# 21 matmuls on zeros in place of twelve ahead of the first product of the context

## The chip, the cores and the metric

The kernel runs on one core of a Trainium2 chip. The metric is the device time of one execution in microseconds (us); the figure to compare is the median of several executions. Before the change it is 1860.94 us, the median of three executions (1864.06, 1858.99 and 1860.94).

Five engines work side by side, each through its own instructions in order: TensorE (PE in the profile) multiplies, VectorE (DVE) and ScalarE (ACT) read and write SBUF and PSUM, GpSimd (POOL) works in SBUF, SyncE (SP) issues DMAs. An instruction that needs another engine's result carries a wait on a semaphore, and everything behind it on its own engine stands still until that wait ends.

## The reference, cut to what matters

The reference defines four sets of attention, but the context has just the 77 text positions, so the kernel computes cross-attention over those: 32 batches of 512 queries, 20 heads of 32 columns.

```
q = heads(x @ to_q_w)                      # x: 32 x 512 x 640
k = heads(ctx @ to_k_w)                    # ctx: 32 x 77 x 1024
v = heads(ctx @ to_v_w)
p = softmax(q k^T / sqrt(32))              # per head, over 77 keys
out = merge(p v) @ to_out_w + to_out_b + x
```

Float32 is required, so each operand is split into a high part and a rest, and each product is three matmuls (high by high, high by rest, rest by high).

## The kernel before, in words

**Keys and values of the whole context.** The 32 x 77 = 2464 rows of the context are cut into five groups: four of 512 rows and a last one of 416. The 1024 input columns are eight slices (index k), the 640 output columns five chunks (index j). One accumulator of keys or values, `pk` or `pv`, is one chunk of one group; it takes 8 x 3 matmuls (L204) and fills one PSUM bank. VectorE turns the context slices (L171), ScalarE and VectorE split them (L179, L183) and the weights (L103, L104).

**The first group** goes slice by slice, as the weights land: `first` (L339 to L354) runs, for one slice, 15 matmuls of keys (five chunks) and nine of values (three chunks). Eight accumulators are open at once. In groups 1 to 3 a whole group's keys are made in a row, and its values chunk by chunk. Finished values are turned by VectorE (`turn_values`, L256) into one of two buffers `vs` by turns, split there (L262, L266) and stored to DRAM by four DMAs (L271); finished keys are split (L225, L229) and stored (L235). The keys and values of the last groups are part of the next stage.

**The attention** runs by a list of tokens for each batch (`FILL`, `PLAN`, `LAST_`), which says in which order each step is issued; the order on every engine is the order of the tokens. `FILL` (L789) starts with the last values of group 3 (tokens YV, L204, tile `pv`), then has the keys of the last group (YJ, tile `pk`: digits j and k), the first query product (Yq, L542, tile `pq`) and the last group's values (YC), mixed with the first scores (L577), exponentials (L602), and so on. The token YJ30 is chunk 3, slice 0. It stands between YJ22 and YJ11. Among the SP tokens, Yx0 (the load of the second batch's `x`, L302) stands ahead of Ys20, the first of four stores of value chunk 2.

**The PSUM banks.** There are eight. Up to group 3 all `pk`, `pv` and the tile `warm` come from one pool of eight (L139), and which bank a new accumulator gets is decided while the program is recorded, by a timetable that the recorder keeps of its own; the order of instructions is fixed by hand (L327). From the last group on the banks are handed to new pools (`open_banks`, L437; `bank_of`, L429) by name: key chunk 3 and the first query accumulator each inherit one certain bank, and the first matmul into it has to wait until the accumulator that stood there before has been read.

**The matmuls on zeros.** Ahead of everything TensorE runs L336 and L337: a tile `zero` is set by VectorE, and matmuls of 128 x 512 on it write a tile `warm`, which nobody reads.

## Time and profile before

| what | value |
|---|---|
| median of three executions | 1860.94 us |
| the profiled execution | 1860.52 us |
| its span, first to last instruction | 1858.7 us |
| PE busy in the span | 1843.8 us (99%) |
| DVE, ACT, POOL busy | 1563.8, 1524.9, 1301.7 us |
| mean clock granted to TensorE | 0.999 of full |
| matmuls | 10332 |

The stages by time: matmuls on zeros 1.45 to 6.21 us; group 0 from 8.28 us; groups 0 to 3, keys and values, to 227.2 us; the start of the attention to about 380 us; from there the steady part. A row of the timeline has start, length, engine, line, operation, output and inputs, shape and count; in brackets is how long the engine sat idle ahead of it and what ended that. A matmul's length includes its tail, so consecutive ones overlap. A row of stretches has, per engine, busy time and count, then the clock granted to TensorE (PEclk, 1.00 is full speed), the DMA share and GB/s.

### The profile page before, as it was taken

Reading aid. Unit: us, or ns where it says so; the run is one execution under the profiler, and the core shown is the slowest. Engines: PE = TensorE matmul, PEld = TensorE weight load, DVE = VectorE, ACT = ScalarE, POOL = GpSimd, SP = SyncE. Lnnn points to the kernel's source line nnn. Section 1 sums busy time; section 2 is a strip of 40 time slices with the busy share of each in tenths; the row PEclk is TensorE's granted clock in tenths of the full one; section 3 lists DMA queues with packets and bytes.
Section 4 is the critical chain, followed back from the end, with each engine's and each line's share of the span. In section 5 each row is a group of like instructions: output and inputs, shape, how many; then the busy total and the mean of one; then the engine's idle time right before and its main releaser. Section 6 shows DMA issues by size and latency. Waiting matters only on the chain.

```text
span 1858.7 us, 37494 instructions
## 1 busy us (share of the span) xinstructions
PE 1843.8 (99%) x10332; PEld 1656.9 (89%) x10332; DVE 1563.8 (84%) x2502; ACT 1524.9 (82%) x6218; POOL 1301.7 (70%) x1120
## 2 busy tenths in 40 slices
PE   9999999999999999999999999999999999999999
PEld 7888897889999999999999999999999999999998
DVE  5444458899999999999999999999999999999996
ACT  3232248999999999999999999999999999999984
POOL 1100158787887787777778777887788878877874
PEclk9999999999999999999999999999999999999999
DMA  9879779889898888989988989899899988888875
GB/s 186 197 196 251 179 189 261 248 244 243 238 243 242 238 239 227 246 236 232 247 236 240 240 239 242 234 236 245 231 236 247 242 239 240 232 236 240 237 219 192
DMA packets 563295, 431.37 MB, mean 232 GB/s; under 512 B 191120, under 2 KB 471120, under 8 KB 563088
## 3 DMA queue, kind: packets, MB, share of 16 engines
q1 hardware_dynamic: 558192, 413.16, 84.6%
q0 software_dynamic: 4800, 15.65, 2.6%
q8 instruction: 85, 1.39, 0.3%
q14 instruction: 122, 1.00, 0.2%
q10 hardware_dynamic: 96, 0.16, 0.0%
HBM read 247.17 MB, written 181.64 MB: 231 GB/s over the span
## 4 chain that ended last, share of the span: by engine, by line
PE 93%; ACT 2%; DMA 1%; DVE 1%; SPq 1%; issue 1%; POOL 0%; DVEq 0%; ACTq 0%; POOLq 0%
PE po L750 30%; PE pq L542 28%; PE pa L694 12%; PE sc L577 11%; PE pk L204 6%; PE pv L204 6%; ACT pn L602 1%; DMA pd<-z 1%; SPq L531 0%; SPq L633 0%; DVE z L624 0%; POOL xt L320 0%; DMA v_dram<-vs 0%; DVE pp L672 0%; DMA cs<-in_ctx_dram 0%
## 5 line engine op out<-in xcount | busy, mean ns | idle before, releaser
L602 ACT ACTIVATE pn<-sc,nm 128x77 f32<-128x77 f32 x2560 | 795.8, 342 | 39.5 <-DVE nm L588 33.1
L750 PE MATMUL po<-wo_s,at 128*128 128x320 f32 x3840 | 708.1, 311 | 0.1
L750 PEld LDWEIGHTS po<-wo_s,at 128*128 128x128 f32 x3840 | 620.1, 189 | 41.5 <-DVE xr L765 0.6
L542 PE MATMUL pq<-xt,wq_s 128*128 128x512 f32 x2400 | 597.5, 394 | 1.1 <-DVE qt L787 0.8
L602 ACT ACTIVATION_READ_ACCUMULATOR pn<-sc,nm 128x1 f32 x2560 | 567.2, 222 | 0.0
L542 PEld LDWEIGHTS pq<-xt,wq_s 128*128 128x128 f32 x2400 | 436.6, 188 | 80.9 <-ACT pn L602 1.2
L617 POOL TENSOR_TENSOR pn<-pn,rs 128x1232 f32<-128x1232 f32 x160 | 388.0, 2425 | 91.2 <-DVE rs L612 87.5
L694 PE MATMUL pa<-pp,vb 128*128 128x512 f32 x960 | 341.6, 404 | 3.7 <-DVE at L731 2.0
L577 PEld LDWEIGHTS sc<-kb,qt 128*128 128x128 f32 x1920 | 303.9, 188 | 16.6 <-ACT pn L602 2.3
L588 DVE TENSOR_REDUCE nm<-sc 128x4 f32<-128x308 f32 x640 | 295.2, 466 | 23.0 <-PE sc L577 18.9
L577 PE MATMUL sc<-kb,qt 128*128 128x154 f32 (+1 forms) x1920 | 302.7, 274 | 2.7 <-ACT pn L602 1.9
L783 POOL CAST qt<-qt 64x512 fp32r<-64x512 f32 x320 | 196.8, 615 | 142.2 <-ACT qt L779 127.3
L712 DVE TENSOR_TENSOR pa<-pa,aw 64x512 f32<-64x512 f32 x320 | 222.1, 694 | 50.1 <-ACT aw L708 42.7
L624 DVE STREAM_TRANSPOSE z<-pn 128x1280 f32<-128x1280 f32 x160 | 241.1, 1507 | 14.1 <-DMA pd<-z 8.1
L679 POOL TENSOR_TENSOR pp<-raw,pp 64x512 fp32r<-64x512 f32 x160 | 206.7, 1292 | 64.7 <-ACT pp L661 56.1
L708 ACT COPY aw<-pa 64x1024 f32<-64x1024 f32 x160 | 162.1, 1013 | 88.4 <-PE pa L694 87.5
L787 DVE TENSOR_TENSOR qt<-pq,qt 64x512 fp32r<-64x512 f32 x320 | 216.6, 677 | 6.0 <-ACT qt L779 1.1
L320 POOL TENSOR_TENSOR xt<-xs,xt 128x512 fp32r<-128x512 f32 x160 | 203.6, 1300 | 20.0 <-ACT xt L316 15.2
L743 POOL TENSOR_TENSOR xr<-xr,bias 128x640 f32<-128x640 f32 x128 | 202.6, 1584 | 14.2 <-DMA xr<-in_x_dram 3.9
L672 DVE TENSOR_TENSOR pp<-raw,pp 128x1024 fp32r<-128x1024 f32 x160 | 196.2, 1226 | 0.0
L694 PEld LDWEIGHTS pa<-pp,vb 128*128 128x128 f32 x960 | 174.0, 189 | 14.9 <-ACT pp L663 2.8
L663 ACT CAST pp<-raw 128x1024 fp32r<-128x1024 f32 x160 | 168.5, 1053 | 1.0 <-DMA raw<-pd 1.0
(46 smaller groups left out, 1584.8 us busy)
## 6 DMA issues: line engine op xcount, KB each, us to landing
pd<-z SPq DMA_DIRECT2D x640, 160.0 KB, 3.3
raw<-pd SPq DMA_DIRECT2D x160, 512.0 KB, 4.5
xr<-in_x_dram SPq DMA_DIRECT2D x128, 320.0 KB, 3.8
out_dram<-xr SPq DMA_DIRECT2D x127, 320.0 KB, 3.7
xs<-in_x_dram SPq DMA_DIRECT2D x124, 320.0 KB, 5.9
raw<-pd SPq DMA_DIRECT2D x160, 128.0 KB, 4.1
v_dram<-vs SPq DMA_DIRECT2D x80, 192.0 KB, 4.1
k_dram<-ks POOLq DMA_DIRECT2D x20, 512.0 KB, 4.3
```

The costliest lines, as they stand in the source:

```text
L204: nc.tensor.matmul(held[j][:, :gn], w[:, k, a, :], cts[g, k][:, c, :gn], start=(k == 0 and n == 0), stop=(k == NK - 1 and n == 2),)
L542: nc.tensor.matmul(pqs[n], wq_s[:, k, a, j * P : (j + 1) * P], xts[b, k][:, c, :], start=(k == 0 and m == 0), stop=(k == NC_ - 1 and m == 2),)
L577: nc.tensor.matmul(sc[:, cols], qt[:, m, t * P : (t + 1) * P], keys_, start=(m == 0), stop=(m == 2),)
L588: nc.vector.tensor_reduce(nm, sc[:, :KCOLS].rearrange("p (h k) -> p h k", k=NKEY), AX.X, ALU.max, negate=True)
L602: nc.scalar.activation(pnb[n % 2][:, at, :NKEY], sc[:, i * NKEY : (i + 1) * NKEY], AF.Exp, bias=nm[:, i : i + 1], accum_out=sms[n][:, at : ...
L617: nc.gpsimd.tensor_tensor(pf, pf, rs.unsqueeze(2).to_broadcast([P, NQ * HPC, NKEY]), ALU.mult)
L624: nc.vector.transpose(z.rearrange("p b t j -> p t b j"), pn.rearrange("p (t h) k -> p t (h k)", t=NQ).rearrange("p t (b i) -> p t b i", i=Q),)
L679: nc.gpsimd.tensor_tensor(pp[64:, 4, :], raw[:64, 2, :], pp[:64, 4, :].bitcast(F32), ALU.subtract)
L694: nc.tensor.matmul(pas[n][:, p, :], vb[:, p, t, :], pp[:, c, :], start=(c == p), stop=(c == p + 2),)
L712: nc.vector.tensor_tensor(pa[64 * p : 64 * p + 64, 0], pa[:64, p], aw[:, p], ALU.add)
L750: nc.tensor.matmul(pos[b, t, h][:, :HALF], ats[b * NC_ + j][:, a, t * P : (t + 1) * P], wos[0][:, j, c, h * HALF : (h + 1) * HALF], start= ...
L787: nc.vector.tensor_tensor(qt[rows, 1 + w, :], pqs[n][rows], qt[rows, 0, :].bitcast(F32), ALU.subtract)
```

## The change

One number changes.

```
-    for _ in range(12):
+    for _ in range(21):
         nc.tensor.matmul(warm, zero[:, :P], zero, start=True, stop=True)
```

The order of the instructions on DVE, ACT, POOL and SP is the same in both programs, and so is what they wait for, except that counts of finished matmuls are higher by nine. On PE two places differ.

The first is the start of PE's program: the matmuls on zeros, then the first key products of group 0 (`wk_s_88` holds chunks 0 to 2 of the key weights).

```order
 L1123 UNCONDITIONAL_BRANCH [waits barrier_Pool_Activation_PE_DVE_SP_release]
 L337 MATMUL warm<-zero 128x512 [waits DVE_49]
-L337 MATMUL warm<-zero 128x512 x11
+L337 MATMUL warm<-zero 128x512 x20
 L204 MATMUL pk<-ct,wk_s_88 128x512 [waits Activation_49]
 L204 MATMUL pk<-ct,wk_s_88 128x512 [waits DVE_49] x2
```

Nine more matmuls stand ahead of the first product; it waits for ScalarE as it did.

The second place is the keys of the last group, in the start of the attention. Rows with `wk_s_89` are key chunks 3 and 4, and the first of these is YJ30. `DVE_49` is VectorE's count of finished work.

```order
 L204 MATMUL pk<-ct,wk_s_88 128x416 [waits Activation_49]
 L204 MATMUL pk<-ct,wk_s_88 128x416 x5
-L204 MATMUL pk<-ct,wk_s_89 128x416 x3
+L204 MATMUL pk<-ct,wk_s_89 128x416 [waits DVE_49]
+L204 MATMUL pk<-ct,wk_s_89 128x416 x2
 L204 MATMUL pk<-ct,wk_s_88 128x416 x3
 L204 MATMUL pk<-ct,wk_s_88 128x416 [waits Activation_49]
```

No instruction moved, but the first matmul of key chunk 3 now waits for VectorE. Further on, at the end of this run of keys, stands the first matmul of the first query accumulator.

```order
 L204 MATMUL pk<-ct,wk_s_89 128x416 x3
 L204 MATMUL pk<-ct,wk_s_88 128x416 [waits Activation_49]
-L204 MATMUL pk<-ct,wk_s_88 128x416 [waits DVE_49]
-L204 MATMUL pk<-ct,wk_s_88 128x416
+L204 MATMUL pk<-ct,wk_s_88 128x416 x2
 L204 MATMUL pk<-ct,wk_s_89 128x416 x3
 L204 MATMUL pk<-ct,wk_s_88 128x416 x3
-L542 MATMUL pq<-xt,wq_s 128x512 [waits DVE_49]
+L542 MATMUL pq<-xt,wq_s 128x512
 L542 MATMUL pq<-xt,wq_s 128x512 [waits Pool_49]
 L542 MATMUL pq<-xt,wq_s 128x512
```

The query accumulator no longer waits for VectorE. In the built programs the count waited for is the same, 185: before it stands on the first matmul into `pq`, and now on YJ30, 54 matmuls sooner. Count 185 is VectorE's turn of value chunk 4 of group 3 (L256, token Yt4). The reason is the bank: with the longer run of matmuls on zeros the recorder's timetable gives most accumulators from the first group on another bank, and value chunk 4 of group 3 stands in bank 3, which key chunk 3 inherits, where it stood in bank 4, which `pq` inherits. Three waits in between (value counts 177, 182 and 184) are gone, since they are lower counts of the same engine.

## Prediction

> **What bounds the kernel now.** I read the page first, for the engine that sets the end.

> ```profile
> span 1858.7 us, 37494 instructions
> PE 1843.8 (99%) x10332; PEld 1656.9 (89%) x10332; DVE 1563.8 (84%) x2502; ACT 1524.9 (82%) x6218; POOL 1301.7 (70%) x1120
> ...
> PE 93%; ACT 2%; DMA 1%; DVE 1%; SPq 1%; issue 1%; POOL 0%; DVEq 0%; ACTq 0%; POOLq 0%
> ```

> TensorE is busy for 1843.8 of 1858.7 us and makes 93% of the chain that ended last: what delays it delays the end, unless it would have waited later anyway. So next came the stretches in which it has no gap, and the list of what it waited for (in total, times, longest).

> ```profile
> 13.52:227.20 213.68, 213.68 (x944) 177.07 (x943) 101.69 (x166) 62.51 (x114) 16.20 (x24) 1.00 0.86 207
> 380.00:1840.00 1460.00, 1459.98 (x8503) 1329.52 (x8502) 1333.48 (x2134) 1341.69 (x5601) 1160.34 (x972) 1.00 0.89 239
> ```

> ```profile
> PE pk L204 <- ACT wk_s L103: 2.1, 1, 2.1
> PE pa L694 <- DVE at L731: 2.0, 4, 0.9
> PE sc L577 <- ACT pn L602: 1.9, 1, 1.9
> ...
> PE pa L694 <- ACT pp L663: 1.2, 1, 1.2
> PE pq L542 <- DVE qt L787: 0.8, 1, 0.8
> PE sc L577 <- POOL qt L783: 0.7, 1, 0.7
> ```

> From 13.52 to 227.20 and from 380 to 1840 us PE has no gap, at full clock. The first wait is that for the first weights, ahead of which the change puts work. The five others shown, 2.0+1.9+1.2+0.8+0.7 = 6.6 us, lie outside those stretches. So only the first 13 us and the start of the attention can react.

> **The start: nine more matmuls.** The rows of PE, then the clock in slices of half a microsecond:

> ```profile
> 1.45 4.76 PE L337 MATMUL warm<-zero 128*128 128x512 f32 x12 [1.45 <-DVE zero L334]
> 8.28 5.40 PE L204 MATMUL pk<-ct,wk_s 128*128 128x512 f32 x15 [2.07 <-ACT wk_s L103]
> 13.52 2.20 PE L204 MATMUL pv<-ct,wv_s 128*128 128x512 f32 x9
> 15.56 3.56 PE L204 MATMUL pk<-ct,wk_s 128*128 128x512 f32 x15
> ...
> 31.88 3.56 PE L204 MATMUL pk<-ct,wk_s 128*128 128x512 f32 x15
> ```

> ```profile
> 8.50:9.00 0.50, 0.50 (x2) 0.29 (x1) 0.50 (x3) 0.04 (x1) 0.00 (x0) 0.63 1.12 275
> 11.50:12.00 0.50, 0.50 (x3) 0.40 (x2) 0.10 (x1) 0.36 (x1) 0.00 (x0) 0.50 1.35 170
> 12.00:12.50 0.50, 0.50 (x3) 0.42 (x3) 0.50 (x1) 0.00 (x0) 0.00 (x0) 0.96 1.40 171
> ```

> Soon after the gap of 2.07 us the clock is half, from 8.63 us (0.63 over a slice is 0.13 us at full and 0.37 at half) to 12.04 us (0.96 is 0.04 us at half): 3.41 us. The nine matmuls of 13.52 take 15.56-13.52 = 2.04 us, 0.227 each at full clock; nine more on zeros would then end at 1.45+4.76+2.04 = 8.25 us, just ahead of the release at 8.28, so I take it that the clock stays full. Fifteen products at 0.227 are 3.40 us where 5.24 were (8.28 to 13.52): 1.84 us less. Not all of that is kept:

> ```profile
> 9.06 0.29 PEld L204 LDWEIGHTS pk<-ct,wk_s 128*128 128x128 f32 x1 [0.18 <-DVE wk_s L104]
> ```

> ```profile
> 30.91 0.56 DVE L104 TENSOR_TENSOR wk_s<-wraw,wk_s 128x384 fp32r<-128x384 f32 x1 [1.36 <-ACT wk_s L103]
> ```

> The third product needs VectorE's rest of the weights, 9.06 us at any clock, so thirteen products follow from there: 9.06 and some 0.1 to the matmul, plus 13 x 0.227 = 2.95, is 12.1, and 13.5-12.1 = 1.4 us. Then slice 4's key weights come too late to keep it all: VectorE's rest, behind ScalarE's high part and the load, ends at 30.91+0.56 = 31.47. The third product of that slice can start at 31.6 at the earliest; it starts at 31.88 + 2 x 0.227 = 32.33 now. That leaves **0.7 us**. Bounds: nothing, if those weights come 0.7 us later; 1.4 us, if they come sooner.

> [...]

> **The start of the attention: one wait, 54 matmuls sooner.** The order shows that YJ30 now waits for VectorE's turn of value chunk 4, for which the first query product waited. When each happens:

> ```profile
> 228.09 14.24 PE L204 MATMUL pk<-ct,wk_s 128*128 128x416 f32 x75 [0.21 <-ACT xt L316]
> 242.41 0.97 PE L542 MATMUL pq<-xt,wq_s 128*128 128x512 f32 x3
> ```

> ```profile
> 227.26 0.69 DVE vs L256
> ...
> 233.23 3.81 POOL xt L320 x3
> ...
> 237.06 0.32 SPq L302
> ...
> 237.43 4.09 DMA v_dram<-vs
> ...
> 241.64 0.73 DVE vs L256
> ...
> 257.15 0.62 PE sc L577 x3
> ...
> 258.37 2.56 ACT pn L602 x16
> ```

> The chain of waits says why the turn is late: it writes a buffer `vs` whose former content goes to DRAM by a store issued at 237.43 (landed 4.09 us later), behind a load of `x` on SP, which waited for GpSimd's last rest of `x` at 233.23+3.81. The turn ends at 241.64+0.73 = 242.37. Nothing of this waits for PE's keys: the chain goes back through ScalarE and VectorE to the turn of value chunk 2 at 227.26, ahead of all keys. So stalling PE neither delays nor hastens it, and it moves with PE's 0.7 us.

> In PE's 75 keys, 21 stand ahead of YJ30 and 54 from it to the query. They ran from 232.08 on, beneath the wait:

> ```profile
> 232.08:242.16 10.08, 10.08 (x55) 9.90 (x54) 2.72 (x4) 2.19 (x4) 6.01 (x5) 1.00 0.90 199
> ```

> The start 232.08 is 228.09+0.25 for the first, and 20 x 0.187 (10.08/54). Now PE stands from about 232.3 to 242.41 (less 0.7) and runs the 54 after that: **10.1 us**. Bounds: 10.3 (242.41-232.08, had they no cover at all) and 9.1, if the store lands a microsecond sooner. Behind the waiting matmul queue all other keys; ScalarE's and VectorE's splits of finished keys (L225, L229), their stores and the key loads wait for these, and the query accumulator, its copies and the first scores come later by the same.

> Does a later wait take it back? From 242.41 the chain runs through query products and keys to the first scores at 257.15 and the exponentials at 258.37, and from those through probabilities to the later waits of PE. All of it hangs on the delayed products, so the 6.6 us move along. I take nothing back; the bound is all 6.6.

> **The clock after the stall.** PE idle for 10.1 us is more than the 2.07 that cost it the clock at the start. What half clock costs is bounded by the stretch above: 3.41 us at half do the work of 1.7. If the stretch in which PE resumes is busy enough, only its rest is slow, half of 3.41 on average; if not, the next is slow as well: 1.7 to 5.1 us at half, 0.85 to 2.55 lost. I take **1.7 us**, one whole stretch, as at the start.

> **The sum.** 10.1 + 1.7 - 0.7 = +11.1 us. On the profiled execution's 1860.52 (span 1858.7 and 1.8 around it) it is 1871.6; the median is 1860.94, so I predict 1872.0 us, 0.6% slower. A measurement of this kernel can tell about 0.3% from no change, 5.6 us.

> **The rivals.**
> - *The delay is taken back.* If PE's later waits of 6.6 us hung on work that isn't late, 11.1-6.6 = +4.5: 1865.4 us. For it: ScalarE and VectorE are idle for most of 232 to 242 and could run ahead. Against: they lack scores to work on until 257.
> - *The wait is met in time*, on the other side: not slower. If the turn of chunk 4 were done before YJ30, only the start counts: 1860.9-0.7 = 1860.2 us. It decides at 232.1 us: the store of chunk 2 would have to land 10 us sooner, so be issued ahead of the load of `x`, but SP's order is unchanged. The same time results if the recorder's wait were not on this turn.
> - *More than one price.* Keys stored later make key loads and scores later still, or PE loses the clock once more in its later waits: another 1.7 us, 1873.7 and up to 1875.4 for two.
> - *No clock to win at the start.* In an execution whose clock does not fall after the gap of 2.07 us the nine matmuls win nothing: 10.1+1.7 = +11.8, 1872.7 us. Against: the one execution traced did fall. [...]

> **How the numbers follow.** Forecast 0.71, taken back 0.09, met in time 0.05, more than one price 0.09, no clock to win 0.06. The forecast's own ends are 9.1+0.85-1.4 = +8.6 and 10.3+2.55-0 = +12.9; the executions shown lie from 1.95 below to 3.12 above their median. That gives 1860.94+8.6-1.95 = 1867.6 to 1860.94+12.9+3.12 = 1877.0, which holds the forecast, the clock rival and the dearer one; the two others, 0.14, are left out. Slower by over 5.6 us: 0.71+0.09+0.06 = 0.86. Within: 0.13, the first two rivals, less 0.01 for faster by over 5.6 us, for which no row has a price.

> **What would show it.** After: the matmuls on zeros end within 0.1 us of the first product; PEclk is 1.00 there; slice 4 starts some 0.7 us sooner than 31.88. In the start of the attention PE's list of waits has a new first row, about 10 us, `pk` on VectorE's `vs` (L256), once, at about 232 us; PEclk is 0.50 at 242 us for some 3 us; the query product follows the keys at once, 11 to 12 us later than 242.41. From 390 us on the two traces run parallel. I am wrong if that wait is short, if the later waits of PE shrink by several microseconds, or if the stretch from 390 us to the end has another length.

## The result, and the profile after

The changed kernel takes **1873.33 us** (median of six executions, 1871.81 to 1877.14), the one before 1860.52 us beside it (six, 1858.99 to 1864.06). The ratio is 1.0062, 95% interval 1.0050 to 1.0074. In a second comparison (after_again, below) it was 1.0059 (1.0046 to 1.0072). 1872.0 us had been predicted, between 1867.6 and 1877.0.

The page of the changed kernel (the profiled execution took 1872.93 us):

```profile
span 1871.2 us, 37512 instructions
PE 1849.4 (99%) x10341; PEld 1660.9 (89%) x10341; DVE 1561.3 (83%) x2502; ACT 1526.8 (82%) x6218; POOL 1303.0 (70%) x1120
...
PE 90%; DMA 3%; ACT 2%; DVE 1%; SPq 1%; POOL 1%; issue 1%; DVEq 0%; ACTq 0%; POOLq 0%
```

The span is 12.5 us longer, and PE is still 99% busy: the share says nothing. The chain does: PE lost 3% of it, and DMA gained 2%. PE's list of waits of the changed kernel names the place (in total, times, longest):

```profile
PE pk L204 <- DVE vs L256: 9.9, 1, 9.9
PE sc L577 <- ACT pn L602: 1.9, 1, 1.9
PE pq L542 <- DVE qt L787: 1.5, 2, 0.9
```

The first row is new. The other two stood there before, at 1.9 and 0.8 us, but 0.9 of the third row's 1.5 us is a wait at a place where before has none (303.39 us). In total the later waits have shrunk a little: from the first query product to 381 us (times of before) PE stood still for 6.7 us before (138.65 less 131.95 busy) and for 5.3 in the changed kernel (139.42 less 134.13). PE's timeline of the changed kernel, at the start and at the last group's keys:

```profile
1.46 7.40 PE L337 MATMUL warm<-zero 128*128 128x512 f32 x21 [1.46 <-DVE zero L334]
8.70 3.56 PE L204 MATMUL pk<-ct,wk_s 128*128 128x512 f32 x15
12.10 2.20 PE L204 MATMUL pv<-ct,wv_s 128*128 128x512 f32 x9
14.14 2.20 PE L204 MATMUL pk<-ct,wk_s 128*128 128x512 f32 x9
...
30.46 3.56 PE L204 MATMUL pk<-ct,wk_s 128*128 128x512 f32 x15
...
226.65 4.19 PE L204 MATMUL pk<-ct,wk_s 128*128 128x416 f32 x21 [0.19 <-ACT xt L316]
240.70 12.60 PE L204 MATMUL pk<-ct,wk_s 128*128 128x416 f32 x54 [9.86 <-DVE vs L256]
253.14 0.85 PE L542 MATMUL pq<-xt,wq_s 128*128 128x512 f32 x3
...
303.39 0.96 PE L542 MATMUL pq<-xt,wq_s 128*128 128x512 f32 x3 [0.91 <-DVE qt L787]
```

Four steps of the sum are in these rows. The second slice starts at 14.14 (15.56 before), slice 4 at 30.46 (31.88), the last group's keys at 226.65 (228.09): 1.4 us ahead of the profile of before, and kept. YJ30, the first of the 54, starts at 240.70 after 9.86 us of nothing; before it started at 232.08. And the 54 take 253.14-240.70 = 12.44 us, where they took 242.41-232.08 = 10.33: 2.1 us more, for the same matmuls. The clock tells why (the changed kernel, in slices):

```profile
8.50:9.00 0.50, 0.50 (x4) 0.42 (x3) 0.21 (x1) 0.24 (x1) 0.00 (x0) 1.00 1.18 361
...
235.00:235.50 0.50, 0.00 (x0) 0.00 (x0) 0.00 (x0) 0.00 (x0) 0.49 (x1) 0.70 0.93 174
240.50:241.00 0.50, 0.30 (x1) 0.30 (x2) 0.15 (x1) 0.00 (x0) 0.00 (x0) 0.50 1.11 255
245.00:245.50 0.50, 0.50 (x3) 0.47 (x3) 0.00 (x0) 0.00 (x0) 0.00 (x0) 0.56 0.00 0
```

PEclk, the third number from the end, is 1.00 at the start, where it was 0.63. It falls to a half at 235.20 (0.70 over a slice is 0.2 us at full), while PE stands, and rises at 245.44 (0.56 is 0.06 us at full): 4.74 us at half after work resumed.

The chain of waits of the changed kernel shows the way to YJ30:

```profile
231.79 3.71 POOL xt L320 x3
235.51 0.32 SPq L302
...
235.88 3.93 DMA v_dram<-vs
...
239.93 0.73 DVE vs L256
```

These are the pieces of before, GpSimd's rest of `x`, the load of `x`, the store of value chunk 2, the turn of chunk 4, each 1.4 to 1.7 us sooner. What hung on the turn before was the query product; now it is 54 key matmuls.

### The profile page after: what moved, and what is told of

Same layout as the page of the kernel before. It is cut to its first block, busy times and chain, and to the rows that moved or that the text cites. A ratio compares the mean times of both kernels' runs of the same rounds, so it can differ in the third digit from the quotient of the medians.

```text
span 1871.2 us, 37512 instructions
## 1 busy us (share of the span) xinstructions
PE 1849.4 (99%) x10341; PEld 1660.9 (89%) x10341; DVE 1561.3 (83%) x2502; ACT 1526.8 (82%) x6218; POOL 1303.0 (70%) x1120
## 4 chain that ended last, share of the span: by engine, by line
PE 90%; DMA 3%; ACT 2%; DVE 1%; SPq 1%; POOL 1%; issue 1%; DVEq 0%; ACTq 0%; POOLq 0%
PE po L750 28%; PE pq L542 27%; PE pa L694 11%; PE sc L577 10%; PE pk L204 7%; PE pv L204 6%; ACT pn L602 1%; DMA pd<-z 1%; DMA v_dram<-vs 1%; DVE z L624 1%; SPq L633 0%; PE warm L337 0%; SPq L512 0%; DMA wo_s<-wo_dram 0%; POOL pn L617 0%
## 5 line engine op out<-in xcount | busy, mean ns | idle before, releaser
L602 ACT ACTIVATE pn<-sc,nm 128x77 f32<-128x77 f32 x2560 | 797.4, 343 | 39.3 <-DVE nm L588 33.1
L542 PE MATMUL pq<-xt,wq_s 128*128 128x512 f32 x2400 | 598.6, 394 | 1.7 <-DVE qt L787 1.5
L602 ACT ACTIVATION_READ_ACCUMULATOR pn<-sc,nm 128x1 f32 x2560 | 568.6, 222 | 0.0
L542 PEld LDWEIGHTS pq<-xt,wq_s 128*128 128x128 f32 x2400 | 437.2, 189 | 81.6 <-DVE qt L787 1.1
L694 PE MATMUL pa<-pp,vb 128*128 128x512 f32 x960 | 342.2, 404 | 2.6 <-DMA kb<-k_dram 0.9
L577 PEld LDWEIGHTS sc<-kb,qt 128*128 128x128 f32 x1920 | 304.3, 189 | 16.5 <-ACT pn L602 2.2
L577 PE MATMUL sc<-kb,qt 128*128 128x154 f32 (+1 forms) x1920 | 303.3, 274 | 2.2 <-ACT pn L602 1.9
L783 POOL CAST qt<-qt 64x512 fp32r<-64x512 f32 x320 | 197.6, 617 | 153.9 <-ACT qt L779 138.9
L624 DVE STREAM_TRANSPOSE z<-pn 128x1280 f32<-128x1280 f32 x160 | 241.2, 1507 | 17.2 <-DMA pd<-z 10.1
L787 DVE TENSOR_TENSOR qt<-pq,qt 64x512 fp32r<-64x512 f32 x320 | 216.8, 677 | 6.5 <-ACT qt L779 1.7
L320 POOL TENSOR_TENSOR xt<-xs,xt 128x512 fp32r<-128x512 f32 x160 | 203.6, 1298 | 20.1 <-ACT xt L316 15.2
L672 DVE TENSOR_TENSOR pp<-raw,pp 128x1024 fp32r<-128x1024 f32 x160 | 195.4, 1221 | 0.2 <-ACT pp L663 0.2
L694 PEld LDWEIGHTS pa<-pp,vb 128*128 128x128 f32 x960 | 173.9, 189 | 14.4 <-ACT pp L663 1.7
L663 ACT CAST pp<-raw 128x1024 fp32r<-128x1024 f32 x160 | 168.5, 1053 | 1.3 <-DMA raw<-pd 1.3
```

The source lines that it names most:

```text
L542: nc.tensor.matmul(pqs[n], wq_s[:, k, a, j * P : (j + 1) * P], xts[b, k][:, c, :], start=(k == 0 and m == 0), stop=(k == NC_ - 1 and m == 2),)
L577: nc.tensor.matmul(sc[:, cols], qt[:, m, t * P : (t + 1) * P], keys_, start=(m == 0), stop=(m == 2),)
L602: nc.scalar.activation(pnb[n % 2][:, at, :NKEY], sc[:, i * NKEY : (i + 1) * NKEY], AF.Exp, bias=nm[:, i : i + 1], accum_out=sms[n][:, at : ...
L624: nc.vector.transpose(z.rearrange("p b t j -> p t b j"), pn.rearrange("p (t h) k -> p t (h k)", t=NQ).rearrange("p t (b i) -> p t b i", i=Q),)
L694: nc.tensor.matmul(pas[n][:, p, :], vb[:, p, t, :], pp[:, c, :], start=(c == p), stop=(c == p + 2),)
L787: nc.vector.tensor_tensor(qt[rows, 1 + w, :], pqs[n][rows], qt[rows, 0, :].bitcast(F32), ALU.subtract)
```

## The experiments

**One matmul more: thirteen.** The smallest change that moves the banks in the built programs.

```
-    for _ in range(12):
+    for _ in range(13):
```

> Thirteen matmuls on zeros in place of twelve. Theory (what costs time is the recorder's other bank for value chunk 4 and with it the wait on YJ30, not the matmuls): the built program has YJ30 waiting for count 185, as with 21, so the wait of about 10 us is there, and half clock after it; the start gains nothing or little, since the thirteenth ends about 6.4 us and a gap of 1.8 us is left. About 1872.5 to 1875 us, 12 to 14 above the kernel before. Rival (the nine matmuls themselves, or their load on the clock, cost the time): one ninth of it at most, about 1861 to 1862 us.

Measured 1873.36 us (1871.61 to 1874.67, four executions), ratio 1.0065 (1.0049 to 1.0080). PE's timeline:

```profile
1.45 5.40 PE L337 MATMUL warm<-zero 128*128 128x512 f32 x13 [1.45 <-DVE zero L334]
7.66 4.02 PE L204 MATMUL pk<-ct,wk_s 128*128 128x512 f32 x15 [0.81 <-ACT wk_s L103]
...
241.15 12.22 PE L204 MATMUL pk<-ct,wk_s 128*128 128x416 f32 x54 [10.01 <-DVE vs L256]
253.20 0.86 PE L542 MATMUL pq<-xt,wq_s 128*128 128x512 f32 x3
```

One matmul of 0.2 us on data that nobody reads costs as much as nine. The loss is none of the work added; it is the wait at YJ30. That the banks make it is read in the built programs (they differ in this from twelve matmuls to thirteen); the trace shows the wait. One part of the theory missed: the start was to gain little, but the weights came at 7.66 us here, the gap was 0.81 us and not 1.8, and the second slice started at 13.56, sooner than with 21 (14.14).

**Key chunk 3 later: late_chunk3.** With 21 matmuls on zeros, YJ30, YJ31 and YJ32 go behind the first query product.

```
-YJ22 YJ30 YJ11 ... YJ25 YJ31 YJ07 YJ32 YI0 YJ17 Yi0 Yq0 Yl3
+YJ22 YJ11 ... YJ25 YJ07 YI0 YJ17 Yi0 Yq0 YJ30 YJ31 YJ32 Yl3
```

> 21 matmuls on zeros, and the first three slices of key chunk 3 (YJ30, YJ31, YJ32) issued behind the first query product instead of among the other keys; the banks are those of the changed kernel. Theory: YJ30 is reached about 240 us and waits under 1 us, the clock stays full, and the start's 1.4 us are left: 1859 to 1860.5 us, equal to the kernel before or 1 us below it. Rival (the lost time does not come from this wait): about 1873 us.

Measured 1862.12 us (1859.50 to 1865.82, twelve executions), ratio 1.0004 (0.9994 to 1.0014). PE's timeline:

```profile
227.22 12.67 PE L204 MATMUL pk<-ct,wk_s 128*128 128x416 f32 x66 [0.91 <-ACT xt L316]
...
241.41 4.23 PE L204 MATMUL pk<-ct,wk_s 128*128 128x416 f32 x21 [0.81 <-DVE vs L256]
```

The wait is 0.8 us instead of 9.9, and the 12.8 us are gone. So the whole loss hangs on that wait, the half clock included. But the gain of the start, which was to bring 1859 to 1860.5 us, is not seen at the end; two runs below ask where it went.

**The stall kept busy: filled.** 50 key matmuls whose results are discarded (the accumulator is started anew afterwards) stand ahead of YJ10, between the first 12 keys and YJ30. The wait stays, but PE works through it, and the run shows what the clock does then. The loop, without the lines around it:

```
+                for _ in range(50):
+                    nc.tensor.matmul(
+                        pks[1][:, :416], wk_s[0][:, 0, 0, :P], cts[LAST, 0][:, 0, :416], start=True, stop=True
+                    )
```

> The changed kernel with 50 more matmuls (128 x 416) issued into the bank of key chunk 1 just before its first real product, which starts the bank anew, so they end before YJ30's wait does. Theory: the wait of 9.9 us is nearly filled (0.3 to 0.7 us are left), YJ30 starts at the same 240.7 us, but the clock stays at 1.00, so the 54 keys take 10.1 us and not 12.4: the time falls by about 2.1 us, and by up to 1.7 more if the later drop of the clock goes too: 1869.5 to 1871.2 us. Rival (the clock after the wait costs nothing, the keys would have waited for something else): 1873.3 us.

Measured 1873.55 us (1872.80 to 1874.60, four executions), ratio 1.0068 (1.0050 to 1.0085): not the gain that was expected, but the time of the rival. PE's timeline (L1017 is the filling):

```profile
229.31 9.59 PE L1017 MATMUL pk<-ct,wk_s 128*128 128x416 f32 x50
238.73 1.86 PE L204 MATMUL pk<-ct,wk_s 128*128 128x416 f32 x9
241.24 10.44 PE L204 MATMUL pk<-ct,wk_s 128*128 128x416 f32 x54 [0.65 <-DVE vs L256]
251.52 0.86 PE L542 MATMUL pq<-xt,wq_s 128*128 128x512 f32 x3
```

At the place itself the theory holds: the 54 keys take 251.52-241.24 = 10.28 us, as before the change (10.33), and the query product is 1.6 us sooner than in the changed kernel. What follows takes it back. In the changed kernel and in filled, PE stands behind the kernel before by 10.7 and 9.1 us at the first query product, by 11.2 and 10.5 us at 327 us (times of before), by 11.5 and 11.3 us at 381 us. PE's waits of filled say on what:

```profile
PE pa L694 <- DVE at L731: 2.6, 3, 1.2
PE sc L577 <- ACT pn L602: 2.2, 1, 2.2
PE pq L542 <- DVE qt L787: 1.8, 2, 1.2
```

The changed kernel has 0.8, 1.9 and 1.5 us there (of the 2.6, one wait of 1.1 us lies at the very end). The two lower rows alone make 0.6 of the 1.4 us: here VectorE and ScalarE set part of the pace, and a PE that comes sooner waits longer. What is left at 381 us is 0.2 us, and 0.5 at the end, less than the executions scatter. So the half clock's 2.1 us are real at their place, and little of them reaches the end.

**The store first: store_first.** Ys20, the first store of value chunk 2, ahead of the load of `x` on SP.

```
-Yu3 Yu0 Yx0 Ys20 Yx2
+Yu3 Yu0 Ys20 Yx0 Yx2
```

> The changed kernel with the first store of value chunk 2 (Ys20) issued on SP ahead of the load of x (Yx0) instead of behind it. Theory (the turn that YJ30 waits for is late because of this store): the store goes out about 2 us sooner (233.7 instead of 235.9), the turn of value chunk 4 ends about 2 us sooner and the wait is 7.5 to 8 us instead of 9.9: 1870.8 to 1871.8 us. Rival (another store or engine sets the turn): no change, 1873.3 us.

Measured 1871.98 us (1870.84 to 1874.44, four executions), ratio 1.0059 (1.0044 to 1.0075), 0.2 us over the expected range. The chain of waits, then PE's timeline:

```profile
231.46 1.15 SPq L271
...
233.68 0.90 SPq L271
234.63 3.60 DMA v_dram<-vs
238.75 0.71 DVE vs L256
```

```profile
239.51 12.43 PE L204 MATMUL pk<-ct,wk_s 128*128 128x416 f32 x54 [7.88 <-DVE vs L256]
```

The wait is 2.0 us shorter, so the store is what the turn waits for, and the load of `x` was ahead of it on SP. No more than that, because SP now issues store after store at about 1 us each. At the end 0.6 us (by the ratio) to 1.4 us (by the median) are seen of it, which the intervals don't tell from nothing.

**What the start is worth: reordered_12 and no_zeros.** reordered_12 is late_chunk3 with the twelve matmuls of before; no_zeros has none, and nothing else changed.

```
-    for _ in range(12):
+    for _ in range(0):
```

> Twelve matmuls on zeros as before, but key chunk 3 of the last group (its first three slices) stands behind the first query product, as in late_chunk3. Nothing of the computation changes. Theory: the reordering by itself costs nothing, because PE has other keys to run in the meantime; the start is as before, so the time is that of the kernel before within 1 us, 1861 to 1863 us beside its 1861.9, and late_chunk3's start gain of 1.4 us went into its two short waits (0.9 and 0.8 us) and into clock losses that come and go from execution to execution. Rival: the reordering itself costs what the start gained, some 1.4 us or more, and the ratio is above 1.0008.

> No matmuls on zeros at all; the product's first wait is still for ScalarE's weights, and by the build key chunk 3 does not wait for VectorE. Nothing of the computation changes. Theory: the first product is released at 8.3 us whatever stands ahead of it, PE starts at half clock and gets the full one 3.4 to 6.8 us later, so it loses 1.7 to 3.4 us where the kernel before loses 1.8: at the second slice it stands 0 to 1.6 us behind before, and the end is 0 to 1.6 us later, 1861.9 to 1863.5 us. No wait of 10 us at key chunk 3. Rival: the number of matmuls on zeros has a price of its own beside the bank (the zeros keep PE's first product waiting), then no_zeros is faster than before at the second slice.

reordered_12 measured 1863.70 us (1860.49 to 1868.18, eleven executions), ratio 1.0012 (1.0003 to 1.0020); no_zeros 1863.86 us (1861.24 to 1866.66, eleven), ratio 1.0010 (1.0001 to 1.0019). The rival won for the first: the reordering by itself costs 0.12%, 2.2 us. PE's timeline of reordered_12:

```profile
228.06 12.67 PE L204 MATMUL pk<-ct,wk_s 128*128 128x416 f32 x66 [0.67 <-ACT xt L316]
242.36 0.96 PE L542 MATMUL pq<-xt,wq_s 128*128 128x512 f32 x3 [1.63 <-DVE vs L256]
```

The nine keys that were moved had filled the time up to the turn of value chunk 4; without them the query product waits 1.6 us for it. The two ratios differ by 0.08%, 1.5 us, about the 1.4 that the trace shows at 227 us, but each interval is about 0.1% wide to a side and they overlap: at the end no gain of the 21 matmuls is told from nothing.

Nor do the traces show that the nine more matmuls are what wins at the start. PE's start in reordered_12, with the same twelve as before:

```profile
7.68 4.03 PE L204 MATMUL pk<-ct,wk_s 128*128 128x512 f32 x15 [0.87 <-ACT wk_s L103]
...
13.59 3.56 PE L204 MATMUL pk<-ct,wk_s 128*128 128x512 f32 x15
```

The weights came 0.6 us sooner than in the profile of before, the gap was 0.87 us and not 2.07, and the clock stayed full (1.00 from 6.53 to 9.94 us). The second slice starts at 13.59, sooner than with 21 (14.14). At 227 us the five profiles with 21 matmuls stand 0.6 to 1.8 us ahead of that of before, and those with eighteen, thirteen, twelve and none 0.3, 1.1, 0.5 and 0.6. The profile of before is the one of the ten with the latest weights.

no_zeros shows how little the start says by itself:

```profile
7.75 5.30 PE L204 MATMUL pk<-ct,wk_s 128*128 128x512 f32 x15 [7.75 <-ACT wk_s L103]
12.88 2.20 PE L204 MATMUL pv<-ct,wv_s 128*128 128x512 f32 x9
```

Its fifteen products take 5.13 us, like the 5.24 of before and not the 3.40 that they took in the changed kernel at the full clock, and its second slice is 0.6 us sooner than that of before, only since ScalarE's weights were there at 7.75 and not at 8.28. This release lies between 7.66 and 8.28 us in the profiles where the product waits for it. So the rival's sign is there, a second slice sooner than that of before, but the weights explain it. The time is 0.4 us over the expected range. At 290 us no_zeros is 2.4 us ahead of before, at 327 us 1.6 us behind.

**All that helped together: both.** Eighteen matmuls on zeros, late_chunk3's order and store_first's.

> Eighteen matmuls on zeros, key chunk 3 of the last group behind the first query product, and the store of value chunk 2 issued ahead of the load of x. Nothing of the computation changes. Theory: no long wait at key chunk 3, the first product at the full clock (second slice 1.4 us or more sooner than 15.56 us), and value chunk 4 turned 2 us sooner, so that the wait of 0.8 us that late_chunk3 had is gone: PE is 1.5 to 2.5 us ahead of before at 290 us. At the end 1859 to 1861 us beside 1861.9, ratio 0.9985 to 0.9995. Rival: between 300 and 335 us ScalarE and VectorE set the pace (PE waits there in every kernel), so what PE gained ahead of them is waited out there and the ratio is 1.000 or above.

Measured 1860.19 us (1857.52 to 1863.41, eleven executions) beside 1861.84, ratio 0.9992 (0.9984 to 1.0001). PE's timeline:

```profile
227.88 12.88 PE L204 MATMUL pk<-ct,wk_s 128*128 128x416 f32 x66 [0.33 <-ACT xt L316]
240.60 0.86 PE L542 MATMUL pq<-xt,wq_s 128*128 128x512 f32 x3
241.29 4.12 PE L204 MATMUL pk<-ct,wk_s 128*128 128x416 f32 x21
```

No wait is left at YJ30. But at 290 us PE is 0.4 us ahead of before and not the expected 1.5 to 2.5: of a lead of 1.95 us at the second slice 0.3 is left at 227 us, since weights hold PE up from slice 4 on (0.5 us of it is one wait for value weights, L103). By its median it is the fastest of all, 1.7 us below before, but its interval just reaches 1: not told from no change.

**The changed kernel once more: after_again.**

> The changed kernel once more, beside the other kernels on one chip. Theory: 1.0062 again (1.005 to 1.0074), with the wait of 9.9 us at key chunk 3; what differs between profiles of the same kernel is where the clock's stretches of 3.41 us fall against the wait of 1.9 us at 324 us: full or half afterwards, 0 to 2 such stretches at half between 310 and 340 us, each worth 1.2 to 1.7 us there. Rival: such a stretch at half belongs to the changed kernel: it has one at 324 us in every execution, and before has none; then it is again one, at the same place.

Measured 1873.14 us (1869.28 to 1875.71, six executions), ratio 1.0059 (1.0046 to 1.0072). Again one stretch at half, 326.32 to 329.73 us, so this run doesn't tell theory from rival: both profiles of the changed kernel have one. Other kernels have such stretches too (below), so they don't belong to the changed one alone. It has one thing of its own:

```profile
241.76 13.20 PE L204 MATMUL pk<-ct,wk_s 128*128 128x416 f32 x54 [9.99 <-DVE vs L256]
254.79 0.85 PE L542 MATMUL pq<-xt,wq_s 128*128 128x512 f32 x3
```

Here the 54 keys take 13.03 us, 2.7 more than at full clock.

## Why the prediction was right, step by step

- **The start gain, 0.7 us predicted (0 to 1.4): 1.4 us between these two profiles, on another path and partly by luck.** The matmuls on zeros took 7.40 us, 0.6 more than worked out: they went from 0.43 to 0.23 us each at about 6.5 us, in before at about 5.2. So the zeros held the first product until 8.70, and not the weights: ScalarE's two casts of them (L103) ended at 7.09+0.82 = 7.91, in before at 7.72+0.81 = 8.53. From 8.70 all fifteen ran at the full clock (12.10-8.70 = 3.40). The working had 12.1 too, but by a third product that waits for VectorE until 9.06; that the two agree is luck. The term that was mis-sized is the limit at slice 4: that slice started at 30.46, its third product 0.45 later, ahead of the 31.6 that the weights of before had allowed, so these came sooner here. In other executions less is kept: at 227 us after_again is 0.8 us ahead of before, store_first 0.6, thirteen 1.1. And how much there is to win depends on the execution of before: reordered_12, with twelve, lost no clock at the start.
- **YJ30's wait, 10.1 us: right.** The 54 keys start 240.70-232.08 = 8.6 us later than before, and would have been 1.4 sooner: 10.0 us. Single waits were 9.9 and 10.0 in the kernels with the same order. thirteen, late_chunk3 and store_first show the cause from three sides.
- **Half clock after the stall, 1.7 us (0.85 to 2.55): 2.1 us**, 1.7 in thirteen, 1.9 in store_first, 2.7 in after_again. The clock did fall in the stall (0.50 from 235.20 to 245.44 us in the changed kernel); after_again is over the upper bound, with 6.05 us at half after work resumed (241.76 to 247.81) where 5.1 was the most allowed for.
- **Nothing taken back of the later waits: right for the 10 us, wrong by 1.4.** PE was 10.7 us behind at the first query product and 10.1 at 291 us (times of before): a wait of 0.7 us for GpSimd was gone. Then the wait of 0.9 us at 303.39, which before does not have, made it 11.2. Why it is there stays open: no_zeros, whose keys are not late, has one of 0.9 us at the same product. Then came another stretch at half clock, 323.95 to 327.36. That is the rival "more than one price", but its price did not last: PE's delay rose to 12.6 us and was 11.2 again at 327 us, since two waits for VectorE that follow in before, 0.89 (shown below) and 0.81 us, were none and 0.55. So of the 6.7 us of later waits 1.4 were taken back in all. filled shows the same for a small gain: there 1.4 us of 1.6 were waited out up to 381 us.
- **The steady part, parallel from 390 us on: right in kind, with 0.9 us more.** The changed kernel is 11.5 us behind at 381 us and 12.4 at the end; 0.7 of that came between 743 and 1152 us. after_again is 12.5 behind at 431 us and 13.0 at the end. What causes these stays open.

The first of the two waits of before that the changed kernel does not have:

```profile
318.25 0.47 PE L694 MATMUL pa<-pp,vb 128*128 128x512 f32 x1 [0.89 <-DVE at L731]
```

The sum by what was measured: -1.4 for the start, +10.0 for the wait, +2.1 for the clock, -0.6 taken back up to 291 us, +1.1 with the wait at 303.39, nothing for the second stretch at half, +1.2 from there on (0.3 of it up to 381 us): 12.4 us, beside 12.5 between the two spans. The two large terms are right. That the sum of 11.1 came within 1.3 us is partly luck: 2.3 us that it did not have are offset in part by 0.7 more at the start and 0.6 taken back. The rival "met in time" did not come true. The condition of "no clock to win", a clock that does not fall ahead of the first product, is met in other executions with few zeros: the gap was 0.81 us in thirteen and 0.87 in reordered_12, and the clock was 1.00 from 6.12 to 9.53 and from 6.53 to 9.94 us.

## What to carry to other kernels

Ahead of any small edit near a pool of rotating buffers, compare what every instruction waits for in the two built programs. Here one matmul of 0.2 us on unused data moved an accumulator to another bank, and a wait that had ended just as the work ahead of it did came 54 matmuls sooner. A change at one end of a program is priced at the place where its waits move, not at the place of the edit. And a microsecond won or lost just ahead of a stretch where other engines set the pace was mostly evened out there (1.4 of the 1.6 us of filled), while the 10 us were not. One profile of each kernel is not enough to price such a microsecond.

## What the runs showed of the hardware

Between the first product and the last the clock granted to TensorE changes at 8.63 and 12.04 us in before and at 235.20, 245.44, 323.95 and 327.36 us in the changed kernel. That is 3.41 us apart in before and 3, 23 and 1 times 3.41 in the changed kernel. Each trace can so be cut into stretches of 3.41 us, and the time that PE was busy in one stretch be put beside the clock of the next. Two neighbouring stretches of before, then of the changed kernel, then of late_chunk3 (PE's busy time is the second number, PEclk the third from the end):

```profile
309.00:312.41 3.41, 1.86 (x12) 1.49 (x10) 3.19 (x8) 3.36 (x15) 3.32 (x6) 1.00 0.84 294
312.41:315.83 3.42, 3.06 (x16) 2.58 (x17) 3.35 (x5) 3.42 (x19) 3.27 (x3) 1.00 1.00 376
```

```profile
320.53:323.95 3.42, 1.56 (x10) 1.26 (x8) 3.17 (x6) 3.37 (x15) 3.33 (x6) 1.00 0.92 315
323.95:327.36 3.41, 3.40 (x9) 2.87 (x10) 3.34 (x5) 3.41 (x19) 3.26 (x3) 0.50 1.02 376
```

```profile
320.15:323.56 3.41, 1.69 (x8) 1.39 (x9) 3.38 (x6) 2.09 (x5) 3.19 (x3) 1.00 0.95 328
323.56:326.97 3.41, 3.41 (x12) 2.73 (x10) 2.89 (x4) 3.21 (x16) 1.28 (x1) 0.50 0.46 169
```

The stretches lie differently against the program in each profile, and between 300 and 340 us a profile has none, one or two at half. That of the changed kernel raised PE's delay from 11.2 to 12.6 us where it lies; how much of it is left differs with the place. In the changed kernel, after_again, filled and both one stretch follows the wait for ScalarE, and PE takes 14.3 us from 313 to 327 us (times of before), as in before and in reordered_12, which have none there: the waits that follow are shorter. In store_first, late_chunk3 and no_zeros a second stretch lies further on, and in thirteen the only one; there PE takes 16.6 to 17.4 us. A wait of 1.2 to 1.7 us for VectorE (L672) that before does not have is part of this. Executions of before differ with the clock too: those beside the last four kernels took 1861.2 us on average at a mean clock of 0.999 (13 of them) and 1863.5 at 0.997 (9). This luck of some 2 us in a single execution is as large as all that the start can win.
